# A depthwise convolution put off through DRAM, smaller norm matrices, and work dealt by estimated times

## The chip, the cores and the metric

The kernel runs on one core of one Trainium2 chip. The metric is the device time of one execution in microseconds (us). The time before is 4386.24 us, the median of three runs (4383.31 to 4386.42). Five engines work side by side, each in the order in which its instructions were written: PE (TensorE, the matrix products), DVE (VectorE), ACT (ScalarE), POOL (GpSimd) and SP (SyncE, which here only issues transfers). POOL issues transfers too.

## The reference

Two layers run over an image of 64 x 64 positions and 256 channels in float32. Only the first layer's convolutions are touched by the change:

```
qkv = concat(conv1x1(x), conv3x3(x), conv5x5(x))     # 256 channels each: q, k, v
qkv = depthwise3x3(qkv)                              # one 3x3 filter for each channel
q, k = l2norm(q), l2norm(k)                          # over the 32 channels of each of 8 heads
attn = softmax(q k^T * temperature);  o = attn v;  out = x + conv1x1(o)
```

After it come a second layer of a state-space scan in two directions, and a mixture of experts. Their code is the same before and after.

## The kernel before

`conv_phase` makes q, k and v and stores them in DRAM (`qd`, `kd`, `vd`); attention loads them from there. The 256 channels are two tiles of 128 partitions (`t`, 0 or 1), the image two halves of 32 rows (`half`). The 3x3 and 5x5 convolutions go by the Winograd method along the rows: the weights of each filter row (`weights`, for k three pieces for each output tile co, in two steps each, for v five pieces in three steps each) are transformed by DVE and sent through DRAM (`uk`, `uv`), the inputs of a half are transformed by DVE (`inputs`) into planes that occupy nine places in SBUF, and PE multiplies (`feed`, L452): a k product is 12 PE instructions, a v product 20, a q product 4.

The work is a list of units in a fixed order: k(0,0), k(0,1), k(1,0), k(1,1) as (half, t), and then q and v in turn: q(0,0), v(0,0), q(1,0), v(0,1), q(0,1), v(1,0), q(1,1), v(1,1). A k unit has six products, taken in three groups of two; a v unit has eight in four groups; a q unit four in one group. `feed` keeps at most three products issued ahead of the one that is used, and issues none whose inputs or weights are not there. `transform_out` takes products in pairs: ACT copies the second (`c`, L481), DVE adds and subtracts (L275, L272) into a padded plane `pad` of which there are two in turn; two ACT copies (`sides`, L504 and L505) complete it.

While unit n's products are made, `depthwise` runs over the plane of unit n-1: a unit of half 0 yields 24 rows and one of half 1 yields 40, since rows 24 to 31 and one beyond are kept in `edge` (L698, L728). For each unit ACT makes the first of nine taps (L524) and DVE the other eight, in two pieces (L528, 16 instructions), into an `acc` buffer; there are three of these in turn. For v, `turn` transposes the result on PE and stores it. For q and k the result goes, in chunks of 8 rows (512 columns), through a norm round of up to three chunks: ACT squares (L550), PE sums over heads with a 128 x 32 matrix (L551), then `norm_inverse` takes the maximum (L558), the square root on ACT (L559) and the reciprocal (L560), PE spreads the result to 128 partitions (L565), and `norm_apply` multiplies (L275) and stores. The three steps are run by `tick`, one step a tick, and one round is under way at a time; a tick comes once in a group of products.

Between groups a fixed number of steps of the waiting transforms is dealt, 5 in a group of k, 4 of q, 3 of v:

```
for g in range(groups):
    step(main)
    feed()
    tick()
    for _ in range(-(-18 // groups)):
        step(before)
    for _ in range(share[kind]):
        step_fill()
    feed()
```

`step_fill` takes the first of a list that can go: inputs of k half 0, weights of k co 1, inputs of k half 1, weights of v co 0, inputs of v half 0, weights of v co 1, inputs of v half 1. Inputs have to wait for three free places; weights don't. Where the product to be used next hasn't been issued, `product` calls `step_fill` until it has. The raw weights come by POOL's queue, one piece at a time, through one buffer (`wr`, L282).

Of the kernel before, what the change touches and what calls it, by code (L numbers as in the profile page):

```python
# [14 lines left out]
FP = mybir.dt.float32  # L15
# [157 lines left out]

def conv_phase(cx, xT, w1, w3, w5, temp, qd, kd, vd, uk, uv):

# [16 lines left out]
    with ExitStack() as ctx:  # L192
# [3 lines left out]
        tp = ctx.enter_context(tc.tile_pool(name="a_t", bufs=6))  # L196
        accp = ctx.enter_context(tc.tile_pool(name="a_acc", bufs=3))
        pcv = ctx.enter_context(tc.tile_pool(name="a_pcv", bufs=4, space=PSUM))
        pms = ctx.enter_context(tc.tile_pool(name="a_pms", bufs=1, space=PSUM))
# [24 lines left out]
        for t in range(CT):  # L224
            nc.sync.dma_start(out=wq[:, t, :], in_=w1[t, 0, :, 0, :])

        heads = one.tile([P, 32], FP, name="heads")
        pick = one.tile([P, P], FP, name="pick")
        nc.vector.tensor_reduce(
            pick.rearrange("p (a b) -> p a b", b=32)[:, :, 0:1], cx.ident.rearrange("p (a b) -> p a b", b=32),  # L230
            AX.X, ALU.add,
        )
        nc.vector.tensor_copy(
            heads.rearrange("p (a b) -> p a b", b=8),
            pick.rearrange("p (a b) -> p a b", b=32)[:, :, 0:1].to_broadcast([P, 4, 8]),
        )
        first_of = one.tile([P, 32], FP, name="first_of")
        nc.vector.memset(first_of, 0.0)
        for h in range(4):
            nc.vector.memset(first_of[:, 8 * h : 8 * h + 1], 1.0)  # L240
        rep = one.tile([P, 4], FP, name="rep")
        for h in range(4):
            nc.vector.tensor_reduce(
                rep[:, h : h + 1], cx.ident.rearrange("p (j a) -> p a j", a=32)[:, 8 * h, :], AX.X, ALU.add
            )
        nc.vector.tensor_copy(pick.rearrange("p (a b) -> p a b", b=32), rep[:, :, None].to_broadcast([P, 4, 32]))

        pick_q = []
        for t in range(CT):
            x = tp.tile([P, 4, 32], FP, name="px", tag="t")  # L250
            nc.vector.tensor_scalar(
                x, heads[:, None, :].to_broadcast([P, 4, 32]), temp[:, t : t + 1], None, ALU.mult
            )
            y = one.tile([P, 4, 32], FP, name=f"px{t}")
            nc.vector.tensor_tensor(y, x, first_of[:, None, :].to_broadcast([P, 4, 32]), ALU.mult)
            ps = pms.tile([P, N], FP, name="ps", tag=f"ps{t}")
            nc.tensor.transpose(ps[:, 0:P], y.rearrange("p a b -> p (a b)"), cx.ident)
            pq = one.tile([P, P], FP, name=f"pick_q{t}")
            nc.vector.tensor_copy(pq, ps[:, 0:P])
            pick_q.append(pq)  # L260

# [7 lines left out]
        UD = {"k": uk, "v": uv}  # L269

        def madd(out, x, f, y):
            nc.vector.scalar_tensor_tensor(out, x, f, y, ALU.mult, ALU.add)  # L272

        def plus(out, x, y, op=ALU.add):
            nc.vector.tensor_tensor(out, x, y, op)  # L275

# [45 lines left out]

        V, free = {}, list(range(9))

        def inputs(kind, half):
# [12 lines left out]
            def stand(i, s):  # L338
                V[kind, half, i] = place[s].rearrange("p (r t j) -> p r t j", t=CT, j=TX)
                where[kind, half, i] = s  # L340

            for a in range(1, 7 if kind == "v" else 5, 2):
# [78 lines left out]
        def feed(depth=3):  # L421
            while at["job"] < len(jobs):
# [17 lines left out]
                if kind == "q":  # L440

                    r, s = 2 + HR * half + 16 * (i // 2), 2 - 2 * (i % 2)
                    for ci in range(CT):
                        nc.tensor.matmul(
                            ps.rearrange("p (h s j) -> p h s j", s=2, j=TX), wq[:, t, P * ci : P * ci + P],
                            xpad[:, r : r + 16, ci, s : s + 2, i % 2 : i % 2 + TX], start=ci == 0, stop=ci == CT - 1,
                        )
                else:
                    k, u, v = KS[kind], us.pop(n), V[kind, half, i]
                    for dy in range(k):  # L450
                        for ci in range(CT):
                            nc.tensor.matmul(  # L452
                                rows4(ps), u[:, dy, P * ci : P * ci + P], v[:, dy : dy + HR, ci, :],
                                start=dy + ci == 0, stop=dy == k - 1 and ci == CT - 1,
                            )
                at["job"] += 1

        def product():
            feed()
            while at["used"] not in ms:  # L460
                assert step_fill()
                feed()
            n = at["used"]
            at["used"] += 1
            (kind, half, t), i = jobs[n]
            if kind != "q" and t == CT - 1:
                free.append(where.pop((kind, half, i)))
            return ms.pop(n)
# [34 lines left out]
        def sides(pad, r0):  # L503
            nc.scalar.copy(pad[:, r0 : r0 + HR, 0, 1:TX], pad[:, r0 : r0 + HR, 4, 0 : TX - 1])  # L504
            nc.scalar.copy(pad[:, r0 : r0 + HR, 5, 0 : TX - 1], pad[:, r0 : r0 + HR, 1, 1:TX])  # L505

        def depthwise(kind, half, t, pad):

            row0, n = (LAG, H - LAG) if half else (0, LAG)
            ch = {"q": 0, "k": CT, "v": 2 * CT}[kind] + t  # L510
            dst = accp.tile([P, (H - LAG) * W], FP, name="acc", tag="acc")

# [12 lines left out]
            for b in range(2):  # L525
                for tap in range(1, 9):
                    o, src, w_ap = piece(b, tap)
                    nc.vector.scalar_tensor_tensor(o, src, w_ap, o, ALU.mult, ALU.add)  # L528
                    yield
                if kind == "v":  # L530
                    turn(dst, t, row0 * W // P, n * W // P // 2 * b, n * W // P // 2)
            if kind != "v":
                c0 = row0 // ROWS
                rows_left.extend((dst[:, N * j : N * j + N], kind, t, c0 + j) for j in range(n // ROWS))
                if not busy:
# [4 lines left out]
        def norm_sums():  # L540
# [6 lines left out]
            ps = pms.tile([P, N], FP, name="ps", tag="ps0")  # L547
            for j, (a, _, _, _) in enumerate(chunks):
                sq = tp.tile([P, N], FP, name="sq", tag="t")
                nc.scalar.activation(sq, a, AF.Square)  # L550
                nc.tensor.matmul(ps[32 * j : 32 * j + 32, :], heads, sq, start=True, stop=True)  # L551
            later(lambda: norm_inverse(chunks, ps))

        def norm_inverse(chunks, ps):

            n = 32 * len(chunks)
            rn = rp.tile([P, N], FP, name="rn", tag="rn")
            nc.vector.tensor_scalar(rn[0:n, :], ps[0:n, :], 1e-24, None, ALU.max)  # L558
            nc.scalar.activation(rn[0:n, :], rn[0:n, :], AF.Sqrt)  # L559
            nc.vector.reciprocal(rn[0:n, :], rn[0:n, :])  # L560
            back = []
            for j, (_, kind, t, _) in enumerate(chunks):
                back.append(pms.tile([P, N], FP, name="ps", tag=f"ps{j}"))
                r = slice(32 * j, 32 * j + 32)
                nc.tensor.matmul(back[j], (pick_q[t] if kind == "q" else pick)[r, :], rn[r, :], start=True, stop=True)  # L565
            later(lambda: norm_apply(chunks, back))

        def norm_apply(chunks, back):
            for (a, kind, t, c), ps in zip(chunks, back):
                plus(a, a, ps, ALU.mult)  # L570
                if kind == "q":

                    s = tp.tile([P, N], FP, name="qo", tag="t")
                    nc.scalar.copy(
                        s.rearrange("p (h j r) -> p h r j", j=TX, r=4), a.rearrange("p (h r j) -> p h r j", r=4, j=TX)
                    )
                    a = s
                nc.gpsimd.dma_start(out=(qd if kind == "q" else kd)[t][:, N * c : N * c + N], in_=a)
            norm_sums()
# [25 lines left out]
        with tc.manual_schedule(engines=ORDERED):  # L605
# [69 lines left out]
            def step_fill():  # L675
# [13 lines left out]
                return False  # L689


            share = {"k": 5, "q": 4, "v": 3}
            before = None
            for n, (kind, half, t) in enumerate(units):
                pad, r0 = pads[n % 2], 9 if half else 1
                edge = edges["q" if kind == "q" else t]
                if half:
                    nc.scalar.copy(pad[:, 0:9], edge)  # L698
# [17 lines left out]
                for g in range(groups):  # L716
# [3 lines left out]
                    for _ in range(-(-18 // groups)):  # L720
                        step(before)
                    for _ in range(share[kind]):
                        step_fill()
                    feed()
                drain(main)
                drain(before)
                if not half:
                    nc.scalar.copy(edge, pad[:, LAG : LAG + 9])  # L728
                before = depthwise(kind, half, t, pad)
            drain(before)  # L730
            while events:
# [1233 lines left out]
def kernel(  # L1965
# [22 lines left out]

    vd = scratch(CT, [P, NB, P], "vd")
    uk = [scratch(4, [P, 3, C], f"uk{co}") for co in range(CT)]  # L1990
    uv = [scratch(6, [P, 5, C], f"uv{co}") for co in range(CT)]
# [20 lines left out]

    conv_phase(cx, xT, w1, w3, w5, temp, qd, kd, vd, uk, uv)
    with tc.tile_pool(name="early", bufs=1) as pool:
# [106 lines left out]
```

## Time and profile before

| what | us |
|---|---|
| median of three runs | 4386.24 |
| the profiled execution, its own time | 4368.56 |
| its span, first to last instruction | 4366.8 |
| busy in the span: PE, DVE, ACT, POOL | 3693.8, 3600.9, 2685.7, 1563.3 |
| first convolution product on PE starts at | 37.2 |
| first q product, first v product start at | 253.6, 311.4 |
| DVE takes the last v product at | 664.2 |
| attention's first scores on PE start at | 730.2 |

The times of single instructions are read from the profiled execution. A line of a timeline has the start, the time, the engine, the line of the kernel, the operation with what it writes and reads, how often it comes in a row, and in brackets the idle time of the engine before it and what ended that idle time. In a line of groups the busy time and the mean time in ns follow the first bar, the idle time before them the second. Some products have two PE instructions in float32, and the ends of pipelined products are modelled by the profiler.

### The profile page before, as it was taken

To read this page: it belongs to the slowest core of one execution; us is meant where nothing else is said; L and a number is where in the kernel's file an instruction comes from. 1 tells how busy PE (TensorE), PEld (TensorE's weight loads), DVE (VectorE), ACT (ScalarE), POOL (GpSimd) and SP (SyncE) were. 2 spreads that over 40 slices of the span, in tenths; PEclk is the share of its full clock that TensorE was granted. 3 is DMA by queue.
4 is the path that set the end of the run, shared out by engine and by line. 5 is a ranking of instruction groups with operands and counts; after the bars stand their busy time and mean duration, and the time that the engine had idled before them with its cause. 6 is when DMAs were issued, how large, how long until landed. Compare 5 with 4: busy or idle time off the path is not lost. (4 is left out here: it accounts for less than half of the span.)

```text
span 4366.8 us, 43278 instructions
## 1 busy us (share of the span) xinstructions
PE 3693.8 (85%) x15072; PEld 1180.6 (27%) x15072; DVE 3600.9 (82%) x2976; ACT 2685.7 (62%) x4175; POOL 1563.3 (36%) x1051
## 2 busy tenths in 40 slices
PE   4659895999999999997878788888788788876698
PEld 2224341222222222222222222222222222221243
DVE  6887876888879879778899999999999999999311
ACT  1012223888788888776677777777777777774122
POOL 2210000000000000002677677776767777776000
PEclk9879996999999999998888989989888898977799
DMA  4322223000000000003332334443323334332121
GB/s 148 125 77 93 75 79 129 4 30 11 25 23 18 16 23 18 11 23 118 104 108 98 103 124 119 123 119 107 127 82 124 124 114 118 120 109 84 63 63 37
DMA packets 150243, 351.18 MB, mean 80 GB/s; under 512 B 35461, under 2 KB 44421, under 8 KB 149502
## 3 DMA queue, kind: packets, MB, share of 16 engines
q1 hardware_dynamic: 139214, 313.17, 23.1%
q0 software_dynamic: 10800, 35.14, 2.3%
q8 instruction: 120, 1.97, 0.2%
q14 instruction: 109, 0.89, 0.1%
HBM read 268.69 MB, written 79.56 MB: 80 GB/s over the span
## 5 line engine op out<-in xcount | busy, mean ns | idle before, releaser
L1669 POOL TENSOR_TENSOR dbx<-dtxr,b 128x1024 f32<-128x1024 f32 x512 | 1205.8, 2360 | 467.7 <-DVE da L1677 320.7
L1677 DVE TENSOR_TENSOR_SCAN da<-da,state,dbx 128x1024 f32<-128x1024 f32 x512 | 1203.2, 2350 | 62.0 <-ACT state L1700 33.6
L960 ACT ACTIVATE e<-sc 128x1024 f32<-128x1024 f32 x1024 | 992.8, 1023 | 204.7 <-PE sc L953 161.2
L881 DVE TENSOR_TENSOR s<-s,e 128x1024 f32<-128x1024 f32 x768 | 880.6, 1216 | 44.7 <-ACT e L960 44.2
L1659 ACT ACTIVATE da<-dtr,aneg 128x512 f32<-128x512 f32 x1024 | 708.3, 692 | 36.0 <-DMA dtr<-dtd 3.8
L953 PE MATMUL sc<-q,kS 32*128 32x512 f32 x4096 | 653.6, 644 | 20.4 <-DMA kS<-kd 11.4
L1682 DVE TENSOR_TENSOR h<-da,c 128x1024 f32<-128x1024 f32 x512 | 627.2, 1225 | 37.7
L888 PE MATMUL av<-e,vT 128*32 128x512 f32 x4096 | 549.8, 608 | 3.7 <-ACT o L894 3.7
L1709 PE MATMUL y<-h,sel 128*32 128x512 f32 x2048 | 442.0, 675 | 130.9 <-DVE h L1682 130.7
L132 POOL TENSOR_TENSOR ln_few<-ln_few,minus_half 128x4 f32<-128x4 f32 x29 | 29.4, 1015 | 1417.8 <-DMA ln_few<-ln_row 1417.8
L452 PE MATMUL cv<-v,u 128*128 128x512 f32 x928 | 422.2, 615 | 64.4 <-DVE pad L272 27.4
L953 PEld LDWEIGHTS sc<-q,kS 32*128 32x128 f32 x4096 | 211.3, 183 | 466.9 <-issue 244.4
L1250 PE MATMUL mm<-u,win 128*128 128x512 f32 x496 | 267.2, 688 | 72.0 <-DMA u<-ud 52.4
L1700 ACT COPY state<-da 128x2 f32<-128x2 f32 x511 | 80.5, 158 | 362.5 <-DVE h L1682 360.0
L452 PEld LDWEIGHTS cv<-v,u 128*128 128x128 f32 x928 | 182.1, 198 | 302.9 <-issue 230.9
L528 DVE SCALAR_TENSOR_TENSOR acc<-pad,wdw_s,acc 128x768 f32<-128x768 f32 (+1 forms) x192 | 244.5, 1279 | 19.4 <-ACT acc L524 13.3
L1294 PE MATMUL mm<-xp,taps 128*128 128x512 f32 x480 | 221.3, 609 | 6.0 <-DVE m L1441 5.1
L881 DVE TENSOR_TENSOR s<-e 128x1024 f32<-128x1024 f32 x128 | 150.8, 1219 | 71.6 <-ACT e L960 71.4
L888 PEld LDWEIGHTS av<-e,vT 128*32 128x32 f32 x4096 | 81.3, 108 | 396.6 <-issue 379.0
L1709 PEld LDWEIGHTS y<-h,sel 128*32 128x32 f32 x2048 | 60.4, 114 | 468.5 <-DVE h L1682 292.8
L1250 PEld LDWEIGHTS mm<-u,win 128*128 128x128 f32 x496 | 104.2, 221 | 244.8 <-issue 127.0
L504 ACT COPY pad<-pad 128x480 f32<-128x480 f32 x12 | 7.1, 594 | 214.2 <-DVE pad L272 214.1
(338 smaller groups left out, 3747.3 us busy)
## 6 DMA issues: line engine op xcount, KB each, us to landing
dtr<-dtd SPq DMA_DIRECT2D x128, 512.0 KB
dtxr<-dtd SPq DMA_DIRECT2D x128, 512.0 KB
b<-bcd SPq DMA_DIRECT2D x64, 256.0 KB
c<-bcd SPq DMA_DIRECT2D x64, 256.0 KB
dtd<-dt SPq DMA_DIRECT2D x64, 256.0 KB
dtd<-few SPq DMA_DIRECT2D x64, 256.0 KB
u<-uv SPq DMA_DIRECT2D x24, 640.0 KB
u<-ud SPq DMA_DIRECT2D x16, 512.0 KB
```

Of the source, the lines that this page charges most:

```text
L452: nc.tensor.matmul(rows4(ps), u[:, dy, P * ci : P * ci + P], v[:, dy : dy + HR, ci, :], start=dy + ci == 0, stop=dy == k - 1 and ci == CT - 1,
L528: nc.vector.scalar_tensor_tensor(o, src, w_ap, o, ALU.mult, ALU.add)
L881: nc.vector.tensor_tensor(z, x, y, ALU.add)
L888: nc.tensor.matmul(g.av[32 * h : 32 * h + 32, :], vT[:, kb, P * t + 32 * h : P * t + 32 * h + 32], es[h // 2][:, h % 2, :], start=kb == 0, ...
L953: nc.tensor.matmul(ps[h // 2][:, h % 2, :], kS[r, t, P * kb : P * kb + P], q_t[r, t, :], start=True, stop=True,)
L960: nc.scalar.activation(e, ps[i], AF.Exp)
L1250: nc.tensor.matmul(ps, win[d][:, t, P * e : P * e + P], u[:, t, ::-1] if d else u[:, t, :], start=t == 0, stop=t == CT - 1,)
L1659: nc.scalar.activation(da[:, v, :], dts[i, e, j][0][:, v, :], AF.Exp, scale=aneg[i % 2][:, a : a + 1])
L1669: nc.gpsimd.tensor_tensor(u, dts[i, e, j][1], bcs[i, k][0][:, None, :].to_broadcast([P, 2, N]), ALU.mult)
L1677: nc.vector.tensor_tensor_scan(da, da, u, state[i % 2][:, 4 * e + j, k : k + 1], ALU.mult, ALU.add)
L1682: nc.vector.tensor_tensor(h, da, bcs[i, k][1][:, None, :].to_broadcast([P, 2, N]), ALU.mult)
L1709: nc.tensor.matmul(ys[i, e][32 * j : 32 * j + 32, :], cx.sel, hs[n + j // 2][:, j % 2, :], start=False, stop=k == SQ - 1,)
```

## The change

It is in `conv_phase` alone, beside the new DRAM tensor `kc` that is handed to it.

Norms: the sums of a chunk are now made with the squares as the stationary operand, four blocks of 128 positions against a 128 x 4 matrix of heads, so that positions lie on partitions and a round of three chunks has 48 columns. Maximum, root and reciprocal work on [128, 48]. ACT spreads each head's value over 32 columns, and four products with the identity turn it back. q's temperature is multiplied in where the norm is applied. The matrices `pick` and `pick_q` go.

Depthwise part of k: a k unit's plane is written to `kc` as soon as it is complete, and there are no edges for k. When both halves of a tile are there, a generator `depthwise_k(t)` is appended to `put_off`. It reads blocks of 16 rows with their neighbours back (`kr`, two buffers, one block ahead) and makes 8 DVE taps of 1024 columns for each; two blocks share an `acc` buffer. In all that is 64 DVE taps, as before (64 of 768 or 1280 columns).

Dealing: `T` keeps two clocks while the program is written, one of PE's products by `COST`, one of DVE's additions, transforms and taps by their columns. `ahead` deals steps until DVE's clock reaches the estimated end of product used+1. `new_acc` gives out an `acc` buffer only if the chunks of its former use are normalised; until then it forces steps of `put_off`, or ticks.

```diff
+        T = {"PE": 0.0, "DVE": 0.0}
+        COST = {"k": 5.2, "v": 8.6, "q": 1.8}
+        def spent(out):
...
+            T["DVE"] += 0.146 + 0.00105 * n
...
# in feed, for every product issued; since = T["DVE"] when its input plane stood
+                done[n] = T["PE"] = max(T["PE"], since.get((kind, half, i), 0.0)) + COST[kind]
# in product
+            T["DVE"] = max(T["DVE"], done[n])
...
+        def step_put_off():
+            while put_off:
+                r = next(put_off[0], None)
+                if r is not None:
+                    return r
+                put_off.pop(0)
+            return False
+        def acc_free():
+            return len(accs) < 3 or not accs[-3]["left"]
+        def new_acc(left):
+            while not acc_free():
+                if not step_put_off():
+                    tick()
+            accs.append({"left": left})
+            return accp.tile([P, (H - LAG) * W], FP, name="acc", tag="acc"), accs[-1]
...
+        def depthwise_k(t):
+            KB = 16
+            def fetch(b):
+                x = kp.tile([P, KB + 2, 6, TX], FP, name="kr", tag="kr")
...
+                nc.gpsimd.dma_start(out=x[:, at0 : at0 + hi - lo], in_=kc[t][:, lo:hi])
+                return x
+            x, dst, log = fetch(0), None, None
+            yield True
+            for b in range(H // KB):
+                if b % 2 == 0:
+                    while not acc_free():
+                        yield False
+                    dst, log = new_acc(2 * KB // ROWS)
+                y = fetch(b + 1) if b + 1 < H // KB else None
+                o = dst[:, KB * W * (b % 2) : KB * W * (b % 2 + 1)]
+                for tap in range(9):
...
+                    if tap == 0:
+                        nc.scalar.activation(o3, src, AF.Copy, scale=w_ap)
+                    else:
+                        spent(o)
+                        nc.vector.scalar_tensor_tensor(o3, src, w_ap, o3, ALU.mult, ALU.add)
+                        if tap % 4 == 0:
+                            tick()
+                        yield True
+                x = y
+                for j in range(KB // ROWS):
+                    rows_left.append((o[:, N * j : N * j + N], "k", t, KB // ROWS * b + j, log))
                 if not busy:
                     norm_sums()
...
-                nc.tensor.matmul(ps[32 * j : 32 * j + 32, :], heads, sq, start=True, stop=True)
+                for i in range(N // P):
+                    nc.tensor.matmul(
+                        ps[:, 16 * j + 4 * i : 16 * j + 4 * i + 4], sq[:, P * i : P * i + P], heads,
+                        start=True, stop=True,
+                    )
...
-            nc.vector.reciprocal(rn[0:n, :], rn[0:n, :])
+            nc.vector.reciprocal(rn[:, 0:n], rn[:, 0:n])
...
-                r = slice(32 * j, 32 * j + 32)
-                nc.tensor.matmul(back[j], (pick_q[t] if kind == "q" else pick)[r, :], rn[r, :], start=True, stop=True)
+                x = tp.tile([P, 16, 32], FP, name="rx", tag="t")
+                nc.scalar.copy(x, rn[:, 16 * j : 16 * j + 16, None].to_broadcast([P, 16, 32]))
+                x = x.rearrange("p (i h) c -> p i (h c)", h=4)
+                back.append(pms.tile([P, N], FP, name="ps", tag=f"ps{j}"))
+                for i in range(N // P):
+                    nc.tensor.matmul(back[j][:, P * i : P * i + P], x[:, i, :], cx.ident, start=True, stop=True)
...
-            share = {"k": 5, "q": 4, "v": 3}
+            def ahead(lag):
+                while True:
+                    n = min(at["used"] + 1, len(jobs) - 1)
+                    end = done.get(n, T["PE"])
+                    if T["DVE"] + lag >= end or not (step_fill() or step_put_off()):
+                        return
+                    feed()
...
-                    for _ in range(share[kind]):
-                        step_fill()
+                    ahead(0.5)
                     feed()
                 drain(main)
                 drain(before)
+                before = None
+                if kind == "k":
+                    nc.gpsimd.dma_start(out=kc[t][:, HR * half : HR * half + HR], in_=pad[:, 1 : HR + 1])
+                    if half:
+                        put_off.append(depthwise_k(t))
+                    continue
                 if not half:
                     nc.scalar.copy(edge, pad[:, LAG : LAG + 9])
                 before = depthwise(kind, half, t, pad)
+            while put_off:
+                step(before)
+                if not step_put_off():
+                    tick()
             drain(before)
             while events:
                 tick()
```

## The prediction

> **What bounds the kernel now.** I read the page's slices first, since the diff edits only the convolution phase.
>
> ```profile
> PE   4659895999999999997878788888788788876698
> DVE  6887876888879879778899999999999999999311
> PEclk9879996999999999998888989989888898977799
> ```
>
> Each digit is 109 us; the phase fills the first six and a half. Then busy time by stretch, cut at the first v product (311.4), the last product (664.2) and attention's first scores (730.2).
>
> ```profile
> 37.20:311.40 274.20, 164.38 (x334) 66.80 (x335) 210.89 (x312) 25.70 (x40) 53.00 (x94) 0.78 0.33 107
> 311.40:664.20 352.80, 327.92 (x811) 139.29 (x809) 276.38 (x253) 76.08 (x114) 20.29 (x42) 0.97 0.23 78
> 664.20:730.20 66.00, 15.37 (x44) 5.44 (x43) 41.23 (x45) 15.29 (x22) 5.97 (x11) 0.54 0.24 83
> ```
>
> Columns: length, then PE, PEld, DVE, ACT, POOL busy, clock, DMA share, GB/s. **A** is bound by DVE and its waits (211 of 274), **B** by PE (328 of 353), **C** is DVE's tail. The groups of the first 900 us:
>
> ```profile
> L452 PE MATMUL cv<-v,u 128*128 128x512 f32 x928 | 422.2, 615 | 64.4 <-DVE pad L272 27.4 <-DMA u<-uk 14.3 <-DVE v L275 13.2
> L528 DVE SCALAR_TENSOR_TENSOR acc<-pad,wdw_s,acc 128x768 f32<-128x768 f32 (+1 forms) x192 | 244.5, 1279 | 19.4 <-ACT acc L524 13.3 <-DVE acc L528 0.5
> L560 DVE RECIPROCAL rn<-rn 96x512 f32<-96x512 f32 (+2 forms) x12 | 40.2, 3348 | 15.3 <-ACT rn L559 15.3
> ```
>
> So a tap is 1.28 us on average, and the reciprocals cost 40. Next DVE's timeline, for what it waits on:
>
> ```profile
> 78.47 0.43 DVE L275 TENSOR_TENSOR wx<-wr 128x256 f32<-128x256 f32 x1 [4.85 <-DMA wr<-in_w]
> 375.33 1.88 DVE L275 TENSOR_TENSOR acc<-acc,ps 128x512 f32<-128x512 f32 x3 [4.96 <-PE ps L565]
> 426.49 1.29 DVE L275 TENSOR_TENSOR out_t<-cv,c 128x512 f32<-128x512 f32 x2 [10.78 <-ACT c L481]
> ```
>
> A weight load that DVE reaches at once is waited for; a norm product queues on PE behind convolution products already issued; ScalarE's `c` queues behind the transposes' copies. Lastly a norm round with nothing beside it, in the tail:
>
> ```profile
> 705.25 1.88 DVE L275 TENSOR_TENSOR acc<-acc,ps 128x512 f32<-128x512 f32 x3 [2.16 <-PE ps L565]
> 711.87 0.68 DVE L558 TENSOR_SCALAR rn<-ps 64x512 f32<-64x512 f32 x1 [4.74 <-PE ps L551]
> 713.25 3.35 DVE L560 RECIPROCAL rn<-rn 64x512 f32<-64x512 f32 x1 [0.70 <-ACT rn L559]
> 718.82 1.29 DVE L275 TENSOR_TENSOR acc<-acc,ps 128x512 f32<-128x512 f32 x2 [2.22 <-PE ps L565]
> ```
>
> Multiply to multiply is 13.6 us, 5 of it DVE at work.
>
> **The norms.** Reciprocal of 48 columns: 0.24 us at 16 columns and 3.35 at 512 in the trace give 0.45; the max falls from 0.68 to about 0.20. Twelve rounds save 12 x 3.38 = 41 us of DVE. PE gets eight instructions a chunk with 128-column weights for the sums (0.12 each by the 1-column sums of L158) and eight of 128 columns back (0.12 by those, 0.165 by the transposes of L587; I take 0.14): 2.1 us a chunk against 0.7 (both products, three chunks in 2.2). ScalarE gets a 512-column copy a chunk, 0.58 to 1.13 by its copies; 0.6 taken. All covered, except in an uncovered round: 13.6 - 3.4 + 0.6 + about 1 = 12 us for three chunks, 7 to 10 for one or two. The dropped set-up is 2 us near 11, when DVE is also fed by xT's loads: nothing taken, at most a gain of 2.
>
> **The k planes through DRAM.** Work on DVE is unchanged: 64 taps of 1024 columns, 1.29 each between the 768 and 1280 column taps (1.03, 1.56). Each of four stores is 1536 KB, each of eight reads 864 KB, on POOL's queue, where the trace has 128 KB in 2.0 us and 640 KB in 4.9; on that line a store is 10.0 and a read 6.2. Attention's loads moved 347 GB/s (724 to 745), so 4.5 for a store bounds it from below. POOL issues in order: a store waits there for ScalarE's two side copies at a k unit's end, and behind it stands the next raw weight load, for which DVE waits. A read stands behind the v weights' stores on POOL; the first tap of a block, on ScalarE, waits for it, and behind that tap ScalarE's other copies. SP's queue gets nothing new. The edge copies of k that go (0.9 us each on ScalarE) were covered.
>
> By the Trainium skill (DMA: Bandwidth & Descriptors, Anatomy of one DMA), a transfer costs 2.0 us and its bytes at 436 GB/s; an estimate by it is 5.6 us a store, and the two loads of A that stand behind a store would come 9 us earlier.
>
> **A.** `ahead` looks at product used+1; where its inputs don't stand yet it gets PE's last end and deals nothing. In k's first unit that is every time, so the next inputs (5.1 us) and co 1's weights come only when `product` demands them. DVE's work to the first v product: 1.4 normalise, k's outputs 4 x 6.8 = 27, inputs 10.3 + 15.5, weights 7.5 + 31.2, eight steps of v's inputs 21: 114 us. Its waits: the first unit's three pairs, 11 + 12 + 9 = 32 (11.0 for the first as now; two products cold are 12.2 for the second); for co 1's three loads 11 + 5 + 5, the first behind a store, then 14 for reload and two cold products (4.3 + 12.9, less 3 worked): 35; v's loads 6 + 12 + 6 + 6 = 30, the 12 behind a store. Sum 97. 37.2 + 114 + 97 = **248 against 311.4: -63**. Out of A go k's taps (58), three norm rounds, and co 1's v weights (31).
>
> **B.** The planner's account, followed with its own constants: its DVE clock T starts with k's first weights (18 x 0.415) and first inputs (4 x 1.288), 12.6, and stands at 156.5 after k. In v(0,0) it deals co 1's v weights (15 steps); the inputs of v half 1 have no free places yet, so four put-off taps follow, one and two more by the end of q(1,0). Then places come free and inputs are dealt, eight of twelve steps by the end of v(0,1). At q(0,1) the depthwise of v(0,1) needs a third buffer back: `accs[-3]` is the one that put-off k began, with 9 of its 16 taps and all of its norms outstanding. `new_acc` forces them there: one tap, then `norm_apply` whose product stands on PE behind three v products just issued (26 us, 24 left to wait); then eight taps and two uncovered rounds, during which PE has nothing fed. T is thereby past PE's last end (341 after v(0,1)'s taps, 347.5 after the first group of v(1,0), against 346.8 for the last product issued), so v(1,0) gets no inputs ahead: its last four products wait for steps that `product` demands, and DVE then waits for the products. DVE work in B: v's inputs 11 + 32, weights 31, v's outputs 44, seven depthwise units 141, 29 put-off taps 37, norms 16: 312. Waits: weight loads 22, first read 8, q(1,0) 18 (as the 10.78 above and a round), q(0,1) 60 (5 + 24 + 6 + 22 + 3 for the buffer's store), v(1,0) 32 (4 + 12 + 16, two lone product pairs), the last units 12: 152. 312 + 152 = **464 against 353: +111**. PE needs 275 + 27 for products, 13 for transposes, 36 for 17 chunks: 351, no bound.
>
> **C.** Dealt by the last product: 7 + 9 forced + 2 in v(1,0) + 11 in v(1,1) = 29 of 64 taps; 35 remain. v(1,1)'s depthwise again needs the put-off buffer: three taps, then three rounds (8 left of the first, 10, 6), the store and first tap 4.5. DVE work: taps 3.9 + 41.3, v's 24.9, 15 chunks 10.2, seven rounds 4.6: 85. Waits: 28.5, 4.5 inside, a last round 11: 44. Then 10 to the first scores, as now (720.1 to 730.2). 139 against 66: **+73**.
>
> Sum -63 + 111 + 73 = +121. The profiled execution took 4368.6 (span 4366.8), the median of the runs is 4386.2, 0.4% above; so 4490 for a profile, and **4507** for the runs. Attention and later are untouched.
>
> PE also cools: 24 instructions took 12.9 at the start and 10.4 late in B, 2.5 us a restart; only the ones named are charged. The skill (TensorE: Matmul & The Clock Gate, Part 1) has the clock halved after about 3.4 us of idleness and for as long; an estimate by it is 1.7 us a restart, and ten more restarts would cost 17 us.
>
> **Rivals.** (1) Faster: the forced taps find their norms done, and idle time stays at today's 172 us (730 - 558). Then DVE's 517 + 172 = 689: -41, **4345**. For it: A does gain, and DVE loses 41 us. Against: the third buffer is asked for at a place fixed in the code. It decides at q(0,1): a wait there under 15 us, and a tail under 100. (2) Milder: rounds overlap better, the stalls of q(0,1), v(1,0) and the tail's 28 cost half: 121 - 60 = +61, **4447**. (3) No change: A's gain pays the tail and B stays at its 353: -63 + 73 = +10 with C as reckoned, -6 with the stores at 4.5: **4386**.
>
> **How the numbers follow.** Some 0.2% (9 us) is what a measurement here can tell from nothing. Main case 0.62 (own range 4465 to 4560: stores at 4.5, with three loads behind them, take off 16, DVE's waits a quarter either way 30 to 50); milder 0.20, all slower; none 0.04; faster 0.14. So faster 0.14, same 0.04, slower 0.82. Leaving out the faster case and a little above, the range is 4385 to 4560.
>
> **What would show it.** Right: the first v product near 248; DVE waiting some 24 us on a norm product near 460, PE idle for tens of us until 545; the last product near 712; over 30 of the 1024-column taps after it; reciprocals of 0.45. Wrong: the last product before 664, or PE over 90% busy through B, would overthrow B's waits; a tail under 100 us, C's rounds; a first v product after 300, A's gain.

## The result and the profile after

The changed kernel takes 4488.65 us (median of four runs, 4483.99 to 4495.36) against 4386.33 us; the ratio is 1.0242, interval 1.0228 to 1.0256. It is slower by 102 us; 4507 had been forecast. Its profiled execution took 4495.36 us. Slices of the page first (each digit 112 us here):

```profile
PE   3788685799999999999787887878888888876698
DVE  4577457788888788868899999999999999999311
PEclk8898786799999999999788998989888988987799
```

The loss lies in the first seven and a half slices: PE and DVE are both less busy there. The digits behind it are nearly those of before. Then the busy time by stretch, cut at the same events: first v product, DVE's last take of a product (here at its end, 712.3; it starts at 711.6), first scores. The columns are length, PE, PEld, DVE, ACT, POOL busy, clock, DMA share, GB/s.

```profile
37.20:248.60 211.40, 145.58 (x304) 62.17 (x305) 111.36 (x176) 10.49 (x19) 32.34 (x56) 0.85 0.38 124
248.60:712.30 463.70, 363.56 (x996) 182.86 (x995) 290.38 (x337) 83.24 (x131) 38.94 (x76) 0.86 0.24 80
712.30:839.10 126.80, 56.71 (x275) 51.90 (x273) 86.08 (x101) 34.27 (x56) 14.78 (x29) 0.57 0.27 92
```

A is 211 against 274, B 464 against 353, C 127 against 66: 109 us up to the first scores. In B neither engine sets the length by work alone; DVE is idle for 173 us of it (76 before). Behind the first scores the code is the same; the two profiles differ there by 18 us (3654.5 against 3636.6). Over all fourteen profiles of this study that part, always the same code, took 3629.7 to 3654.5, so these 18 us are not put down to the change.

The groups of the first 900 us:

```profile
L436 PE MATMUL cv<-v,u 128*128 128x512 f32 x928 | 423.3, 618 | 101.7 <-issue 35.1 <-DMA u<-uk 31.7 <-DVE v L258 13.2
L581 DVE SCALAR_TENSOR_TENSOR acc<-kr,wdw_s,acc 128x1024 f32<-128x1024 f32 x64 | 81.6, 1275 | 26.6 <-ACT acc L578 25.4
L617 DVE RECIPROCAL rn<-rn 128x32 f32<-128x32 f32 (+2 forms) x14 | 5.3, 381 | 17.7 <-ACT rn L616 17.7
```

PE is idle for 101.7 us ahead of the same products, instead of 64.4; the taps cost what they cost before; the reciprocals fall from 40.2 to 5.3. DVE's timeline at the places that the prediction names:

```profile
98.67 0.43 DVE L258 TENSOR_TENSOR wx<-wr 128x256 f32<-128x256 f32 x1 [9.04 <-DMA wr<-in_w]
105.90 0.42 DVE L258 TENSOR_TENSOR wx<-wr 128x256 f32<-128x256 f32 x1 [4.76 <-DMA wr<-in_w]
133.73 1.29 DVE L258 TENSOR_TENSOR out_t<-cv,c 128x512 f32<-128x512 f32 x2 [15.60 <-ACT c L467]
182.97 0.76 DVE L258 TENSOR_TENSOR wx<-wr 128x256 f32<-128x256 f32 x2 [10.57 <-DMA wr<-in_w]
334.66 5.25 DVE L581 SCALAR_TENSOR_TENSOR acc<-kr,wdw_s,acc 128x1024 f32<-128x1024 f32 x4 [9.36 <-ACT acc L578]
478.52 2.54 DVE L632 SCALAR_TENSOR_TENSOR acc<-ps,temp,acc 128x512 f32<-128x512 f32 x3 [23.71 <-PE ps L625]
576.47 1.29 DVE L258 TENSOR_TENSOR out_t<-cv,c 128x512 f32<-128x512 f32 x2 [19.85 <-ACT c L467]
602.57 0.69 DVE L254 SCALAR_TENSOR_TENSOR pad<-cv,out_t 128x512 f32<-128x512 f32 x1 [9.53 <-PE cv L436]
```

The two weight loads of A that stand right behind a store of k are waited for 9.0 and 10.6 us, the other five 4.8 to 7.3; at 478 DVE waits for a forced norm round; at 576 and 602 it waits for products of v(1,0) whose inputs it had not made ahead. PE's side of the forced round:

```profile
451.13 26.46 PE L436 MATMUL cv<-v,u 128*128 128x512 f32 x60
477.43 2.84 PE L625 MATMUL ps<-ident,rx 128*128 128x128 f32 x24
482.72 3.40 PE L605 MATMUL ps<-heads,sq 128*128 128x4 f32 x16 [2.45 <-ACT sq L603]
...
533.89 10.57 PE L436 MATMUL cv<-v,u 128*128 128x512 f32 x20
```

Three v products (60 instructions) stand ahead of the norm's 24; then PE has no v product for 56 us.

### The profile page after: what moved, and what is told of

It is laid out like the page before. It is cut to its first block, busy times and chain, and to the rows that moved or that the text cites. A ratio compares the mean times of both kernels' runs of the same rounds, so it can differ in the third digit from the quotient of the medians.

```text
span 4493.6 us, 44131 instructions
## 1 busy us (share of the span) xinstructions
PE 3746.8 (83%) x15454; PEld 1268.5 (28%) x15454; DVE 3562.7 (79%) x2963; ACT 2697.3 (60%) x4205; POOL 1569.2 (35%) x1063
## 5 line engine op out<-in xcount | busy, mean ns | idle before, releaser
L962 DVE TENSOR_TENSOR s<-s,e 128x1024 f32<-128x1024 f32 x768 | 880.3, 1215 | 45.2 <-ACT e L1041 44.5
L436 PE MATMUL cv<-v,u 128*128 128x512 f32 x928 | 423.3, 618 | 101.7 <-issue 35.1
L536 DVE SCALAR_TENSOR_TENSOR acc<-pad,wdw_s,acc 128x768 f32<-128x768 f32 (+1 forms) x128 | 163.5, 1282 | 14.6 <-ACT acc L531 11.3
L467 ACT COPY c<-cv 128x512 f32<-128x512 f32 x20 | 11.7, 586 | 248.1 <-PE cv L436 203.0
```

The lines of the kernel that those rows point to most:

```text
L436: nc.tensor.matmul(rows4(ps), u[:, dy, P * ci : P * ci + P], v[:, dy : dy + HR, ci, :], start=dy + ci == 0, stop=dy == k - 1 and ci == CT - 1,
L962: nc.vector.tensor_tensor(z, x, y, ALU.add)
```

## The experiments

Each changes the kernel after, unless said otherwise. "First v", "last taken" and "scores" are the three events above, in us of the profiled execution; the ratio is to the kernel before, run beside it on the same chip. The rows from e1 to e4, e5 to e8 and e9 to e11 were each run together; differences across these sets are taken from the ratios, times 4386. e12 was run by itself.

| kernel | first v | last taken | scores | median | ratio (interval) |
|---|---|---|---|---|---|
| before | 311.4 | 664.2 | 730.2 | 4386.33 | 1 |
| after | 248.6 | 711.6 | 839.1 | 4488.65 | 1.0242 (1.0228 to 1.0256) |
| e1_norms | 310.8 | 698.5 | 757.7 | 4403.20 | 1.0057 (1.0040 to 1.0074) |
| e2_inplace | 329.2 | 885.2 | 942.8 | 4585.28 | 1.0467 (1.0450 to 1.0485) |
| e3_shares | 253.2 | 727.2 | 796.8 | 4448.14 | 1.0163 (1.0143 to 1.0183) |
| e4_tailonly | 247.4 | 604.1 | 766.2 | 4416.59 | 1.0091 (1.0074 to 1.0108) |
| e5_look | 208.0 | 635.2 | 730.6 | 4368.42 | 0.9984 (0.9974 to 0.9993) |
| e6_late | 247.7 | 628.6 | 784.7 | 4427.82 | 1.0131 (1.0114 to 1.0148) |
| e7_lateall | 209.5 | 582.6 | 738.5 | 4379.01 | 1.0010 (1.0000 to 1.0020) |
| e8_oldnorms | 210.9 | 572.6 | 764.9 | 4397.73 | 1.0066 (1.0049 to 1.0083) |
| e9_inlook | 280.5 | 731.6 | 789.0 | 4433.05 | 1.0129 (1.0112 to 1.0147) |
| e10_oldinlook | 283.9 | 735.6 | 801.7 | 4445.61 | 1.0153 (1.0136 to 1.0171) |
| e11_eager | 218.5 | 706.8 | 771.0 | 4415.22 | 1.0081 (1.0064 to 1.0098) |
| e12_lookread | 209.4 | 635.0 | 731.5 | 4370.78 | 0.9992 (0.9982 to 1.0002) |

### The three parts of the change by themselves

**e1_norms**, the norms alone: k's depthwise part in place, fixed shares.

```
-                    ahead(0.5)
+                    for _ in range({"k": 5, "q": 4, "v": 3}[kind]):
+                        step_fill()
# and the lines for k after drain(before), and the two that treat k's edges otherwise, taken out
```

> Only the new norms; k's depthwise part in its place, fixed shares of 5, 4 and 3 steps a group. My theory: the loss comes from the dealing and the put-off taps, the norms alone are nearly neutral: DVE is spared 41 us (some 10 in A, 8 in C), PE in B gets about 1.1 us more for each of 21 chunks. First v product near 301, last product near 675, first scores near 730; time -20 to +15 against before. Rival: the norms are the loss (more PE instructions, an uncovered round of 12 us): then +40 or more.

It came out 23 us above the kernel before it was run with (4380.10): above the theory (at most +15) and below the rival (+40 or more). The time is in B (388 against 353), as the waits of DVE there show, of the kernel before and then of e1 (total, times, longest):

```profile
DVE acc L275 <- PE ps L565: 10.4, 3, 5.0
```

```profile
DVE acc L258 <- PE ps L625: 27.6, 7, 17.7
```

PE is busy for 355.7 us of B's 388, against 327.9 of 353: the stretch was bound by PE, and the small products are work there. In B the norm's lines keep PE busy for 39.5 us in e1 and for 18.4 in the kernel before. A norm product waits behind queued v products, and DVE waits for it.

**e2_inplace**, norms and dealing by estimated times, k's depthwise part in place.

```
-                pad, r0 = pads[n % 2], 9 if half and kind != "k" else 1
+                pad, r0 = pads[n % 2], 9 if half else 1
# and the branch that stores k's plane and puts its taps off taken out
```

> New norms and dealing by estimated times, but k's depthwise part stays where it was (no store to kc, no put-off taps). My theory: the dealing costs A some 28 us at co 1's weights, but no buffer is ever held by put-off taps, so q(0,1) waits for nothing long: first v product near 294, last product near 680, first scores near 738; -20 to +35 against before. Rival: the dealing alone is the loss, +60 or more.

Far above both the theory (at most +35) and the rival's bound (+60): 182 us above e1, from which it differs only in the dealing. The waits of PE from 329 to 886 us (total, times, longest):

```profile
PE cv L436 <- DVE v L258: 88.8, 3, 77.5
PE cv L436 <- DMA u<-uv: 51.8, 1, 51.8
PE cv L436 <- DVE v L254: 31.2, 4, 9.5
```

Followed through the code's own constants, the reason is this: with k's taps in place DVE's clock passes PE's by the end of k (166.7 against 159.8), so from there to v(1,0) hardly anything is dealt. Weights and input sums of v are then made one by one when a product asks for them. With k in place, then, the rule of dealing costs 182 us; with k put off it costs 35, as the next run shows.

**e3_shares**, norms and put-off, fixed shares.

```
-                    ahead(0.5)
+                    for _ in range({"k": 5, "q": 4, "v": 3}[kind]):
+                        step_fill() or step_put_off()
```

> New norms and put-off taps through DRAM, but dealt by the old fixed shares (5, 4, 3 steps a group, a put-off tap where no transform can go). My theory: some 50 of the 64 taps are then dealt before the last product and the shared buffer is back in time: first v product near 243, last near 635, first scores near 730; -30 to +25 against before. Rival: putting off through DRAM is itself the loss, whoever deals: +60 or more, with the first tap of blocks waiting for kr.

+68 us, above the theory (at most +25) and 35 below the changed kernel. The rival's figure (+60 or more) is met, its sign hardly: for the first taps of blocks DVE waits 16.7 us in B. A gains as in the changed kernel (217), B is 474. DVE waits in it for norm sums for 45.7 us and for spread-back products for 32.8 and 28.7: shares bring put-off taps early (57 of 64 stand ahead of the last product), and each finished block asks for norm rounds behind v products.

### What the put-off taps cost where they stand

**e4_tailonly**: none dealt between products.

```
-                    if T["DVE"] + lag >= end or not (step_fill() or step_put_off()):
+                    if T["DVE"] + lag >= end or not step_fill():
```

> The changed kernel, but no put-off tap is dealt between products: all 64 come after the last product. My theory: the third buffer is never held in B, so the 60 us of q(0,1) and the 32 of v(1,0) go: first v product near 247 as changed, last product near 610, first scores near 775 since 29 more taps (37 us) come in the tail: about +40 against before, 65 faster than the changed kernel. Rival: the waits in B have another cause (weight loads, PE's longer norms); then B stays at 465 less the 37 us of taps, and the time is that of the changed kernel, +100.

66 us below the changed kernel, as expected. B and C:

```profile
247.40:604.10 356.70, 333.66 (x909) 160.10 (x907) 250.74 (x299) 71.87 (x112) 35.62 (x69) 0.96 0.29 99
604.10:766.20 162.10, 74.24 (x360) 69.26 (x360) 126.17 (x141) 44.96 (x75) 18.25 (x36) 0.57 0.26 89
```

Without those 29 taps B is 107 us shorter and bound by PE again (334 of 357); C is only 35 longer. So the put-off taps, with the third buffer that they hold, are what stretched B in this order of work. Taps and buffer are not told apart by this run.

**e6_late**: put-off taps dealt only once no input sum is left.

```
+                    if ... not (step_fill() or (not fills and step_put_off())):
```

> The changed kernel, but put-off taps of k are dealt between products only once no input sum of a later product is left to deal; the rest of them run at the end. Theory (taps dealt between products while the third accumulator is wanted are what lengthens the stretch of v's products): first v product near 247, the last near 610 to 630 (changed kernel 712, with none dealt 604), first scores near 750 to 770; 4400 to 4425 us, 1.004 to 1.010 times the kernel before. Rival (any put-off tap in the stretch costs its time, wherever it stands): 16 taps of 1.28 us more than with none dealt in the stretch, and nothing won at the end: 4435 to 4450.

4427.82 us, between theory and rival: with 16 taps in it B is 24 us longer than in e4, and C only 6 shorter.

### The dealing's blind spot

**e5_look**: where product used+1 isn't issued, `ahead` gets an estimate of its end.

```
-                    end = done.get(n, T["PE"])
+                    end = done.get(n, T["PE"] + (n - at["job"] + 1) * COST[jobs[n][0][0]])
```

> The changed kernel with one line of its dealing altered: where the next product has not been issued yet, its end is set to TensorE's clock plus the costs of the products up to it, not to TensorE's clock alone; so work is dealt ahead there too. Theory (the dealing does not look past what is issued, and v's input sums for the second half come too late): the 20 us wait for the input sum of v(1,0) falls under 10 us, v(0,0)'s sums come earlier and the first v product at about 230 instead of 248; but put-off taps are still dealt ahead of the third buffer's request, so the waits near 480 for a norm product stay in part. 15 to 60 us below the changed kernel: 4430 to 4475 us, ratio to the kernel before 1.010 to 1.020. Rival (dealing farther ahead only moves put-off taps earlier, and these hold the buffer longer): within 15 us of the changed kernel or above it, 4475 to 4520.

4368.42 us: 113 us below the changed kernel, nearly twice the most that the theory gave, and the only one below the kernel before by more than its interval. The 0.16% is less than the 0.2% that the prediction called telling; the interval lies below 1.

```profile
36.90:208.00 171.10, 144.65 (x305) 61.92 (x306) 119.90 (x198) 10.59 (x19) 36.82 (x64) 0.92 0.48 165
208.00:635.20 427.20, 365.05 (x1037) 187.51 (x1035) 293.97 (x330) 86.79 (x137) 37.05 (x74) 0.89 0.26 90
635.20:730.60 95.40, 45.87 (x232) 42.02 (x232) 74.19 (x88) 30.03 (x49) 11.46 (x22) 0.61 0.27 93
```

A is 40 us shorter and PE is now busy for 145 of its 171, B is 36 shorter, C 31. What the line itself brings forward is inputs and weights: with the put-off taps left under the old rule beside it, the code writes the same order of instructions. The rest follows from that. 16 put-off taps instead of 7 are done when q(0,1) asks for the buffer, so none is forced there, and in C 28 are left instead of 35. v(1,1)'s depthwise gets its buffer at once, so that the forced rounds with which C began (21 us of waits in the changed kernel) are gone. The wait at q(0,1) is still there, and the ones at v(1,0) have shrunk from 44.5 us to 2.5:

```profile
435.04 2.54 DVE L633 SCALAR_TENSOR_TENSOR acc<-ps,temp,acc 128x512 f32<-128x512 f32 x3 [24.31 <-PE ps L626]
```

**e7_lateall**: e5 and e6 together, and k's stores on SP's queue (`nc.sync` for `nc.gpsimd`).

> The two edits together (the dealing looks past what is issued; put-off taps only once no input sum is left), and k's stores to DRAM issued by SyncE instead of GpSimd. Theory: against the kernel with the second edit alone, the two weight waits of 9.0 and 10.6 us behind k's stores fall to 5 to 7 us, the wait of 20 us for v(1,0)'s input sum goes, the first v product comes at 220 to 240: 4375 to 4405 us, 0.998 to 1.005 times the kernel before; still not clearly below it, because the norms in their new form cost TensorE some 25 us. Rival (the stretch of v's products is bound by TensorE either way): first v product earlier, but the last one no earlier than 600, so within 10 us of the kernel with the second edit alone, 4400 to 4425.

4379.01 us, in the theory's range but some 11 us above e5. Against e5, 20 more taps are left for C (48); B is 54 us shorter (373) and C 61 longer (156): the trade that paid in e4 no longer does. The waits for weight loads don't fall as expected: the three of e5 at 135, 151 and 182 us (7.22, 8.84, 7.02) are 7.16, 7.19 and 10.79 here. Only the second of them stands behind a store in e5; the third stands beside one here, though that store is on the other queue.

**e11_eager**: e5 with `ahead(-2.0)` for `ahead(0.5)`.

> The changed kernel with the dealing that looks past what is issued, and with VectorE let 2 us past the next product's end instead of stopping 0.5 us short of it, so that more put-off taps are dealt between products and only 20 of 64 are left for the end. Theory (behind the last product VectorE is what is late, 1.28 us a tap, and the stretch before it has the time): last product at 630 to 650 instead of 630, first scores at 700 to 725 instead of 731; 4340 to 4365 us, 0.992 to 0.998 times the kernel before. Rival (taps dealt earlier hold the third accumulator and delay products, as in the changed kernel): last product at 660 or later, 4370 to 4400.

4415.22 us, the rival's direction and beyond its range; 10 taps are left for C, not 20:

```profile
218.50:706.80 488.30, 383.51 (x1101) 200.34 (x1099) 316.88 (x347) 93.33 (x148) 39.55 (x79) 0.85 0.24 82
706.80:771.00 64.20, 35.25 (x168) 32.13 (x168) 48.98 (x62) 22.91 (x37) 7.59 (x14) 0.56 0.26 93
```

C is 64 instead of 95, but B 488 instead of 427. 18 taps more in B cost 61 us there, 2.6 times their own 23.

**e12_lookread**: e5 with the reads of `kr` on SP's queue and their zero rows set by DVE.

> The changed kernel with the dealing that looks past what is issued, and the reads of the k planes issued by SyncE, whose queue is nearly empty there, instead of GpSimd, where they stand behind the stores of v and of the norms; the zero rows of a block are set by VectorE. The order of all other work is that of the run with the dealing alone. Theory (a read that stands behind stores keeps ScalarE waiting at a block's first tap, 18.5 us once, and VectorE behind it 7.6 us in all): these waits go, 3 to 12 us below the dealing alone, 4355 to 4366 us, 0.995 to 0.998 times the kernel before. Rival (TensorE and the forced norm round set the pace there): within 3 us of the dealing alone, or, where SyncE now stands with a read in front of a weight load, up to 10 us above it.

4370.78 us, the rival. ACT's wait at a block's first tap, of e5 and then of e12:

```profile
ACT acc L579 <- DMA kr<-kc: 18.5, 1, 18.5
```

```profile
ACT acc L579 <- DVE kr L558: 19.4, 1, 19.4
```

Its cause moved and its length stayed: ACT now waits until DVE, in its own order, has set the zero rows. DVE waits for ACT at first taps no less (8.5 us in all against 7.6). Behind the 18.5 us of e5 DVE itself had waited for only 0.45 us, so that little was to be won.

### Is putting k off worth anything, and are the norms?

**e9_inlook**: e2 with e5's line.

> The changed kernel with the dealing that looks past what is issued, and k's depthwise part done in place again as in the kernel before (norms in the new form). Theory (putting k's taps off is what leaves VectorE the time in the stretch of the first products; the new dealing, which deals by VectorE's clock, needs that): first v product near 320 to 340, v's weights and input sums forced one by one behind it; 4400 to 4440 us, 1.006 to 1.015 times the kernel before, so 35 to 75 us above the same dealing with k put off. Rival (the blind spot of the dealing was the only fault, and TensorE's own work of 556 us of the 694 to the first scores decides): within 15 us of the same dealing with k put off, 4350 to 4380.

4433.05 us, in the theory's range, though the first v product comes at 280.5 and not at 320 to 340. e5's line takes 148 us off e2 and still leaves 64 more than with k put off. A:

```profile
36.90:280.50 243.60, 162.82 (x448) 81.98 (x448) 179.06 (x237) 35.05 (x56) 32.52 (x60) 0.82 0.28 91
```

In A DVE does 59 us more than in e5, and PE waits 55.5 us before the first v product, while DVE does, one after the other, the last taps of k (22 us), the rest of the first v weights (27) and the input sum (7). Here the dealing needs the put-off; the kernel before, with fixed shares, doesn't.

**e10_oldinlook**: e9 with the norms of the kernel before. **e8_oldnorms**: e7 with them, and 4 slots instead of 6 in the pool of temporaries, since `kr` leaves no room otherwise.

> The run before with the norms of the kernel before as well, so that of the change only the dealing, looking past what is issued, is left. Theory (the new norms lengthen a stretch bound by TensorE by 25 us, as alone): 15 to 30 us below the run before, 4375 to 4420 us. Rival (here VectorE's forced work is what is late, and the norms in their old form put 41 us more on it): 5 to 40 us above the run before.

> The run before with the norms of the kernel before (one product of 512 columns for a chunk's sums, one for the spread back, the reciprocal on 512 columns); to make room for them the pool of 512-column temporaries has 4 slots instead of 6. Theory (in the stretch bound by TensorE the new form of the norms costs about 1.1 us a chunk more, 25 us in all as in the experiment with the norms alone): 15 to 30 us below the run before, 4350 to 4385 us, 0.992 to 1.000 times the kernel before, with TensorE busy in the stretch of v's products near 310 instead of 335. Rival (what the new norms save on VectorE, 41 us, counts at the end, where VectorE is what is late): 0 to 25 us above the run before, 4390 to 4430.

Both rivals: the old norms are slower by 13 and 19 us by the medians (11 and 25 by the ratios), where the new ones alone had cost 23. In e8 B is 11 us shorter than in e7 (PE busy 323 of 362), and C 36 longer, with nine of the old reciprocals in it (nine of the new ones take 3.3 us in e7):

```profile
L646 DVE RECIPROCAL rn<-rn 64x512 f32<-64x512 f32 (+2 forms) x9 | 30.1, 3346 | 6.3 <-ACT rn L645 6.3
```

Whether the smaller pool has a share in the 19 is open. A fourth `acc` buffer, which would take the forced round away without moving taps, wasn't tried: so how much of B's loss is the buffer and how much the taps stays open.

## Why the prediction was right, and where it was not

**The signs.** Those named for being right came: the first v product at 248.6, a wait of 23.7 us for a norm product, the last product taken at 711.6, 35 taps of 1024 columns behind it, reciprocals of 48 columns in 0.45 us. None of those for being wrong did.

**A: forecast -63, measured -63.** DVE's work 114 forecast, 111 busy (its instructions' own times sum to 121, since neighbours overlap). Waits 97 forecast, 98 measured (100 with those under 0.3 us): the first unit 32 and 33.8; co 1's weights 35 and 34.3; v's loads 30 and 30.3. Loads behind a store: 11 and 12 forecast, 9.0 and 10.6 measured; by the Trainium skill (DMA: Bandwidth & Descriptors, Anatomy of one DMA) the store's 5.6 would have made them about 7 and 8. For these waits the sum, with 10.0 for a store, was nearer; for three of the four stores themselves, which landed after 6.3, 8.1, 6.3 and 6.6 us, the skill's figure was. That the order on POOL's queue alone is the cause is not borne out: in the changed kernel both loads were issued 0.5 us behind the store, and in e7 a load beside a store on SP's queue landed no sooner (the last section has the row).

**B: forecast +111, measured +111, with parts that are off both ways.** DVE's work was given as 312; its groups sum to 303, and it is busy for 290, since neighbouring instructions overlap. The waits were given as 152 and are 173, 167 of it in waits over 0.3 us. That work 22 too high and waits 21 too low cancel is luck; where the waits would stand was not:

| wait | forecast | measured |
|---|---|---|
| weight loads | 22 | 18.9 |
| first read | 8 | 9.4 |
| q(1,0) | 18 | 26.1 |
| q(0,1) | 60 | 47.3 |
| v(1,0) | 32 | 44.5 |
| last units | 12 | 20.9 |

The norm product at q(0,1) was to be waited for 24 us and was for 23.7; the rounds behind it were priced too high, the waits of v(1,0) too low.

**C: forecast +73, measured +61.** 35 taps left over, as forecast; DVE's work 86 against 85. The forced rounds were mis-sized: 21 us of waits instead of 28.5, since the first was half done when C began. For a profile the forecast was 4490, and the profile took 4495: these 12 us less up to the first scores, 18 more behind them, so that it came so near is luck too. The 17 us that the forecast then added for the median, as before, weren't there: this time the median lies 7 us below the profile.

**The norms: "all covered" does not hold where PE binds.** e1, with the dealing of before, shows 23 us. The per-chunk price was near (2.1 forecast, 1.86 measured: 24 instructions in 2.74 and 24 in 2.84 us for three chunks). In the changed kernel PE is busy for 364 of 464 us of B (351 forecast), which leaves room for it; no run has the changed kernel with the old norms, but in the nearest pairs, e7 with e8 and e9 with e10, the old ones are the slower. One reading was loose: in the uncovered round of before DVE is at work for 5.9 of the 13.6 us, not 5; no term rests on it.

**What the runs weigh otherwise.** The prediction gave the buffer at q(0,1) most weight among the waits. e5 takes off 113 us while that wait stays at 24: input sums and weights dealt too late, with what follows from them, were the larger cause. They cost in A too, where the prediction had seen that `ahead` deals nothing and had counted the waits (32 and 35), but inside a stretch that gains in all. Removing the taps (e4, 66), the blind spot (e5, 113) or moving the taps late without the blind spot (e7, 102) shows that these costs don't add. The product demands of v(1,0) show why: they need both the forced taps, which put DVE's clock ahead, and the blind spot, and either edit removes them.

**A restart of PE** was charged 2.5 us. The lone v product at 533.89 takes 10.57 us, a fifth of the 100 instructions from 657.3 on (44.63 us) 8.93: 1.6. Until 537.5, over its first instructions, the granted clock is 0.50, and 1.00 behind that. The estimate by the Trainium skill (TensorE: Matmul & The Clock Gate, Part 1), 1.7, is nearer.

The faster rival (4345) needed a wait under 15 us at q(0,1) and a tail under 100. Neither came. e5 has such a tail (95) with the wait still at 24, and is level with the kernel before. To draw level, the long wait did not have to go: less waiting in A and at v(1,0) and a short tail were enough.

## What to carry to other kernels

A planner that deals by estimated times needs an estimate for exactly the moment when it falls behind; here, stopping where it had none cost 113 us (148 with k in place). Dealing farther than the estimate is no cure: e11 lost some 43 us by it. Work moved out of a stretch bound by one engine returns where another is late, and work that holds a buffer can cost a multiple of its own time. Price an added product on the engine that bounds its stretch, and who waits behind it in that queue, even where the sum of busy times leaves room.

## What the hardware showed that was not expected

- Norm products with 4 moving columns take as long as those with 128: 24 in 2.74 us against 24 in 2.84, each with 128 fresh weight columns.
- A load is slowed by what another queue moves beside it. The 640 KB weight load that POOL issues at 176 us in e5 lands after 6.0 us; while its bytes move (178.0 to 181.4) the DMA engines are busy for 0.60 of the time, at 216 GB/s. In e7 the same load, issued at 174, has a store of k (1536 KB) and loads of transformed weights on SP's queue beside it and lands after 9.7 us; while its bytes move (178.0 to 183.3) the DMA engines are busy for 1.00 of the time, at 408 GB/s.
- The part behind the first scores, the same code in all kernels, took 3630 to 3655 us over the fourteen profiles; differences of some 10 us between single profiles can't be read as the change's.
